# A two-layer metaformer on one core: where the first sample's spectral result is loaded from, and the order of the loads at the seam between two stages

## The chip, the cores and the metric

The kernel runs on one core of a Trainium2 chip, in float32. The metric is device time in microseconds of one execution. Each kernel is run several times and the median is given. Beside that, one execution is recorded by the hardware profiler. Its span goes from the first to the last instruction; its own time is a little longer than the span.

## The reference

The input is 16 samples of 128 channels by 32 x 32 positions. Layer 0 is a linear attention followed by a spectral filter over the 1024 tokens; layer 1 is a pair of 3 x 3 convolutions followed by a routed expert layer.

```python
# layer 0
x = x + attention(ln_c(x))                     # 4 heads, softmaxed q and k, 1x1 projections
t = to_tokens(x)                               # 16 x 1024 x 128
u = ln_t(t)
# spectral part: causal convolution with 16 filters phi (plain and sign-alternated), then a matrix per filter
out = sum_k conv(phi_k, u) @ (s_k * M_phi_plus_k) + sign * conv(phi_k, sign * u) @ (s_k * M_phi_minus_k)
out = out + sum_i shift(u, i) @ M_u_i          # 3 taps
t = t + weighted sum over 4 prefixes of the sequence
# layer 1
x = x + relu(bn2(conv3x3(relu(bn1(conv3x3(ln_c(x)))))) + ln_c(x))
t = t + experts(ln_t(to_tokens(x)))            # 64 experts, each takes its top 8 tokens of each sample
```

## The kernel before

Layer 0's attention and the forward transform of the spectral part run per sample (lines 221 to 774). They leave each sample's spectrum in DRAM (`vd`), its partial result in DRAM (`xd`), and the combined filter matrices in SBUF as `mst` (128 partitions x 32 x 128, 16 KB in each partition), which `filters` builds from 16 loads of `M_phi`.

The **spectral stage** (lines 777 to 921) runs over 16 chunks c of frequencies. `generate` makes the filter matrices of chunk c + 1 with TensorE (stationary `mst`, moving `ph`; line 817), `collect` copies them out of PSUM (828, 830), `multiply` applies those of chunk c to the spectra of all samples (841). In each chunk m runs over 0 to 3, and m takes the parts q = 2m and 2m + 1 of the next chunk's `generate`; part q reads rows 4q to 4q + 3 of `mst`. Each chunk needs spectra `xc`, which `fetch` loads (793) and `turns` on GpSimd turns into `v` (808, 809). `combine` (870, 871) and `finish` (855 to 858) make the results `ys`, and `finish` stores them to DRAM in two stores (862): `yd[0]` holds the 112 rows of chunks 0 to 13, `yd[1]` the 16 rows of chunks 14 and 15. `finish` of chunk c runs in the first step of chunk c + 1, on GpSimd; that of the last chunk runs behind everything, on VectorE. Within `ys` each result of sample 0 sits in 4 partitions for either r, 4 KB in each.

The **convolution stage** (from line 935) takes one sample after the other. Its buffers lie where those of the spectral stage were, and a buffer's first use waits for the last use of what lay there. For sample b, `load` brings x from `xd` and y from `yd` in two parts, 112 rows (896 KB) and 16 rows (128 KB); y has two buffers. Then follow the even and odd classes of the inverse transform (`even`, `odd_t` on GpSimd, 1049 to 1058; `odd_sd`, `odd_turn`, `odd_out` on VectorE, 1062 to 1079), `inverse` on TensorE with `wi` (1133), `add` (1140), tokens, statistics, norm, the product with `tmat` (`terms`, 1173), the transposed image, `ab` (1199), `pair` on GpSimd (1203), and the passes of the first convolution with the matrices `cw` (1013). For all these a planner (`planned`) has written out one order over all samples, with its costs and due times; the instructions of TensorE, VectorE, ScalarE and GpSimd, and SyncE's (SP's) transfers, then stand in that order on each engine. In it, sample 2's `odd_sd` and `odd_turn` stand on VectorE ahead of sample 0's `ab`.

`keep` puts matmuls of the identity, whose result nobody reads, on TensorE: 26 calls, each two instructions of the shape 128 x 256, ahead of the first sample's work (1509).

On SP, the transfers at the seam stand in this order: `gate_w`, `gate_b` (two), `tmat`, `wi`, the four stores of chunks 14 and 15, the last 16 rows of y(0), x(1), y(1), its last 16 rows, the two `cw`, four loads of biases, x(2), y(2) and its last 16 rows. x(0) and the first 112 rows of y(0) go out on GpSimd's queue.

## Time and profile before

| what | value |
|---|---|
| median of 4 runs | 1231.87 us (1226.96, 1227.6, 1236.75, 1236.15) |
| profiled execution: its own time | 1226.96 us |
| profiled execution: its span | 1225.1 us |
| mean granted clock of TensorE | 0.992 |
| TensorE matmuls, busy | 1154.5 us (94%) |
| VectorE / ScalarE / GpSimd, busy | 930.0 / 725.1 / 601.3 us |
| hardware DMA queue | 170.46 MB, 41.2% of 16 engines' span |
| filler matmuls at the seam | from 640.09 us, 11.49 us |
| first step on y(0) | 654.75 us |
| first instruction on y(2) | 675.36 us |
| first two paired convolution passes | from 679.84 us |

Times of single instructions are counted from the span's start. A busy TensorE is not yet a TensorE at its peak, since matmuls are pipelined, and the granted clock is the share of full speed that the array was given. An engine's idle time is put down to whatever ended it; where an instruction waits for several things, it is the last of them. A queue's wait (SPq) is the time in which the next transfer could not be issued; its landing is counted from its issue.

### The profile page before, as it was taken

To read this page: it belongs to the slowest core of one execution; us is meant where nothing else is said; L and a number is where in the kernel's file an instruction comes from. 1 tells how busy PE (TensorE), PEld (TensorE's weight loads), DVE (VectorE), ACT (ScalarE), POOL (GpSimd) and SP (SyncE) were. 2 spreads that over 40 slices of the span, in tenths; PEclk is the share of its full clock that TensorE was granted. 3 is DMA by queue.
4 is the path that set the end of the run, shared out by engine and by line. 5 is a ranking of instruction groups with operands and counts; after the bars stand their busy time and mean duration, and the time that the engine had idled before them with its cause. 6 is when DMAs were issued, how large, how long until landed. Compare 5 with 4: busy or idle time off the path is not lost.

```text
span 1225.1 us, 34369 instructions
## 1 busy us (share of the span) xinstructions
PE 1154.5 (94%) x14376; PEld 946.0 (77%) x14376; DVE 930.0 (76%) x1944; ACT 725.1 (59%) x1420; POOL 601.3 (49%) x800
## 2 busy tenths in 40 slices
PE   7889999999999999999997999999999999998995
PEld 4667767777777999999986888888888888886443
DVE  5888888888776677777764789898898989875235
ACT  4777777776655787877851446555556555644211
POOL 2436454665568788888872434344333333330003
PEclk9999999999999999999998999999999999999998
DMA  7004335253445244444348412233332331406998
GB/s 283 25 31 160 131 99 164 95 160 126 141 135 182 90 141 138 137 141 140 134 153 283 110 52 67 79 96 120 106 119 87 103 103 53 156 35 240 333 403 364
DMA packets 91243, 175.14 MB, mean 143 GB/s; under 512 B 5968, under 2 KB 42064, under 8 KB 90448
## 3 DMA queue, kind: packets, MB, share of 16 engines
q1 hardware_dynamic: 90448, 170.46, 41.2%
q8 instruction: 113, 1.85, 0.6%
q0 software_dynamic: 640, 2.49, 0.6%
q14 instruction: 42, 0.34, 0.1%
HBM read 110.28 MB, written 62.65 MB: 141 GB/s over the span
## 4 chain that ended last, share of the span: by engine, by line
PE 54%; DVE 22%; issue 11%; ACT 6%; DMA 4%; POOL 2%; SPq 0%; POOLq 0%; ACTq 0%; DVEq 0%
PE pcv L1013 10%; PE pg L817 10%; PE py L841 10%; PE big L639 6%; DVE bst L135 4%; PE big L172 3%; PE big L152 3%; PE big L571 3%; PE big L451 2%; PE big L534 2%; PE big L433 2%; DVE abss L1256 1%; DVE xp L1278 1%; DVE xp L1140 1%; ACT ub L550 1%
## 5 line engine op out<-in xcount | busy, mean ns | idle before, releaser
L1013 PE MATMUL pcv<-v,cw 128*128 128x256 f32 x1152 | 258.2, 380 | 0.9 <-POOL v L1203 0.9
L1013 PEld LDWEIGHTS pcv<-v,cw 128*128 128x128 f32 x1152 | 214.7, 190 | 34.0 <-issue 4.9
L830 ACT COPY g<-pg 128x512 f32<-128x512 f32 x316 | 161.1, 605 | 28.3 <-PE pg L817 27.5
L828 DVE COPY g<-pg 128x512 f32<-128x512 f32 x196 | 127.7, 682 | 65.0 <-PE pg L817 65.0
L817 PE MATMUL pg<-ph,mst 32*128 32x128 f32 x4096 | 137.4, 278 | 1.3 <-DVE x L646 0.9
L817 PEld LDWEIGHTS pg<-ph,mst 32*128 32x128 f32 x4096 | 125.1, 186 | 14.7 <-DVE g L828 7.7
L841 PE MATMUL py<-g,v 128*32 128x128 f32 x4096 | 125.1, 274 | 2.5 <-POOL v L809 1.8
L841 PEld LDWEIGHTS py<-g,v 128*32 128x32 f32 x4096 | 108.1, 110 | 10.7 <-POOL v L809 2.3
L144 ACT ACTIVATE tok<-tok,sts 128x128 f32<-128x128 f32 x256 | 101.9, 480 | 16.9 <-DVE sts L1090 13.6
L135 DVE BATCH_NORM_STATS2 bst<-big 128x6 f32<-128x256 f32 x256 | 91.1, 417 | 21.7 <-PE big L152 12.3
L808 POOL TENSOR_TENSOR v<-xc 128x256 f32<-128x256 f32 x128 | 96.9, 781 | 11.0 <-DMA xc<-vd 10.4
L639 PE MATMUL big<-u,mu 128*128 128x128 f32 (+4 forms) x384 | 86.0, 380 | 0.0
L1203 POOL TENSOR_TENSOR v<-abss 128x256 f32<-128x256 f32 x64 | 49.1, 787 | 68.1 <-DVE abss L1199 56.7
L287 POOL TENSOR_TENSOR xf<-ab 128x256 f32<-128x256 f32 x34 | 24.8, 728 | 110.3 <-DVE ab L254 110.2
L1222 POOL TENSOR_TENSOR yo<-abss 128x256 f32<-128x256 f32 x32 | 23.6, 737 | 108.5 <-DVE abss L1218 108.5
L639 PEld LDWEIGHTS big<-u,mu 128*128 128x128 f32 x384 | 56.7, 191 | 18.0 <-issue 15.4
L571 PE MATMUL big<-wf,ub 128*128 128x256 f32 x256 | 62.0, 385 | 0.2
L144 ACT ACTIVATE tt<-tt,sts 128x128 f32<-128x128 f32 x128 | 51.1, 481 | 14.5 <-DVE sts L1090 14.5
L809 POOL TENSOR_SCALAR v<-v 128x256 f32<-128x256 f32 x64 | 55.1, 862 | 5.6
L476 POOL TENSOR_TENSOR ke<-ke,ks 128x1024 f32<-128x1024 f32 x16 | 30.6, 1914 | 55.0 <-DVE qs L484 43.4
L571 PEld LDWEIGHTS big<-wf,ub 128*128 128x128 f32 x256 | 46.2, 190 | 8.8 <-ACT xn L424 3.0
L915 ACT COPY yt<-py 128x512 f32<-128x512 f32 x60 | 35.2, 586 | 29.0 <-ACT g L830 14.9
(256 smaller groups left out, 2481.1 us busy)
## 6 DMA issues: line engine op xcount, KB each, us to landing
we<-in_weight SPq DMA_DIRECT2D x32, 1024.0 KB, 9.2
xc<-vd SPq DMA_DIRECT2D x64, 256.0 KB, 3.0
yd<-ys SPq DMA_DIRECT2D x32, 512.0 KB, 3.8
vd<-xf SPq DMA_DIRECT2D x15, 1024.0 KB, 5.1
y<-yd SPq DMA_DIRECT2D x15, 896.0 KB, 6.3
x<-in_x SPq DMA_DIRECT2D x16, 512.0 KB, 5.3
mi<-in_M_phi SPq DMA_DIRECT2D x16, 512.0 KB, 4.7
xd<-x SPq DMA_DIRECT2D x16, 512.0 KB, 6.4
```

The lines of the kernel that those rows point to most:

```text
L135: nc.vector.bn_stats(bst[:, j : j + 2, :].rearrange("p j s -> p (j s)"), src[:, j : j + 2, :].rearrange("p j c -> p c j"),)
L144: nc.scalar.activation(dst[:, j, :], src[:, j, :], AF.Identity, bias=nm[:, j : j + 1], scale=r[:, j : j + 1],)
L571: nc.tensor.matmul(dst, self.ub[:, q, :], wf[:, q, :], start=True, stop=True)
L639: nc.tensor.matmul(self.pa[:, a:hi], mu[:, NF - 1 - si, tap, :], self.u[:, a - tap : hi - tap], start=(tap == 0), stop=(tap == KU - 1),)
L808: nc.gpsimd.tensor_tensor(vv[:, x, 1:, bs], e, o, op)
L809: nc.gpsimd.tensor_scalar(v[:, :, 0, bs], v[:, :, 2, bs], -1.0, None, ALU.mult)
L817: nc.tensor.matmul(pg[r][:, i], mst[rs, 4 * q + i, :], ph[rs, c, :], start=True, stop=True,)
L828: nc.vector.tensor_copy(dst, src)
L830: nc.scalar.copy(dst, src)
L841: nc.tensor.matmul(py[rows, x, kl, :], v[:, (x * NM + m) * JL + jl, 1 - ri : 3 - ri, :] .rearrange("p k b -> p (k b)"), g[:, ((x * 2 + ri) ...
L1013: nc.tensor.matmul(pc[:, i], wt[:, dy, k, :], v[:, k, dy * WT : dy * WT + HT], start=(dy == 0), stop=(dy == 2),)
L1203: nc.gpsimd.tensor_tensor(v[:, k, WT : WT + HT], self.ab[:, 0], self.ab[:, 1], op)
```

## The change

- `mst` becomes two halves of 16 rows, each with the shape of one y buffer, in a pool `ypool` of two buffers under the tag "y". The y of the convolution stage takes its two buffers from this pool, no longer from `first`. So y(0) lies where rows 0 to 15 of `mst` were, and y(1) where rows 16 to 31 were.
- The first 112 rows of y(0) are loaded by SP within the spectral stage: in chunk 14, step m = 3, behind the last `xc` load.
- `finish` of chunks 14 and 15 copies sample 0's rows straight from `ys` into y(0): four copies of 16 KB for each chunk, ahead of the chunk's stores. Of chunk 15's four, two are issued by ScalarE, all others by SP. The stores of both chunks remain, as the other samples need them.
- x(0) moves from GpSimd's queue to SP, behind the last stores. Then follow the first 112 rows of y(1), x(1), and the last 16 rows of y(1) (before, x(1) stood ahead of y(1)).
- `tmat` moves behind these; `gate_w` and `gate_b` move behind the two `cw`, ahead of the biases.
- `keep` ahead of the first sample's work goes from 26 calls to 13.

```diff
+    ypool = ctx.enter_context(tc.tile_pool(name="ypool", bufs=2, reuse_waits="tile"))
+    yts = {}
+
+    def load_y(b, j0, j1):
+
+        if b not in yts:
+            yts[b] = ypool.tile([P, 2, 2 * NM, C], F32, name="y", tag="y", bufs=2)
+        i = j0 >= P - 2 * JL
+        k = j0 - i * (P - 2 * JL)
+        nc.sync.dma_start(
+            yts[b][j0:j1].rearrange("p r x e -> p r (x e)"),
+            yd[i][k : k + j1 - j0, :, b].rearrange("j r x e -> j r (x e)"),
+        )
...
-        mst = lconst.tile([P, EPR, C], F32, name="mst")
+        mst = [
+            ypool.tile([P, EPR // 2, C], F32, name=f"mst{i}", tag="y", bufs=2) for i in range(2)
+        ]
+
+        def mrow(i, n=1):
+            h, k = divmod(i, EPR // 2)
+            return mst[h][:, k : k + n]
...
-                            pg[r][:, i], mst[rs, 4 * q + i, :], ph[rs, c, :], start=True, stop=True,
+                            pg[r][:, i], mrow(4 * q + i)[rs, 0], ph[rs, c, :], start=True, stop=True,
...
+                for kl in range(JL // RG if c + 2 >= NCH else 0):
+                    for r in range(2):
+                        j0 = P + (c - NCH) * JL + kl * RG
+                        (nc.scalar if kl and c + 1 == NCH else nc.sync).dma_start(
+                            yts[0][j0 : j0 + RG, r].rearrange("p x e -> p (x e)"),
+                            ys[r * B :: 2 * B, kl].rearrange("p x m e -> p (x m e)"),
+                        )
                 for kl in range(JL // RG):
...
                             fetch(c + 2, 0)
+                            if c + 2 == NCH:
+                                load_y(0, 0, P - 2 * JL)
...
-        FIRST = ("wi", "v", "cw0", "cw1", "p1", "y")
+        FIRST = ("wi", "v", "cw0", "cw1", "p1")
...
-            (nc.sync if b else nc.gpsimd).dma_start(xt[b], xd[b])
-            yts[b] = first.tile([P, 2, 2 * NM, C], F32, name="y", tag="y", bufs=2)
-            for i, js in enumerate((slice(P - 2 * JL), slice(P - 2 * JL, P))):
-                (nc.gpsimd if b + i == 0 else nc.sync).dma_start(
-                    yts[b][js].rearrange("p r x e -> p r (x e)"),
-                    yd[i][:, :, b].rearrange("j r x e -> j r (x e)"),
-                )
+            if b != 1:
+                nc.sync.dma_start(xt[b], xd[b])
+            if b:
+                load_y(b, 0, P - 2 * JL)
+            if b == 1:
+                nc.sync.dma_start(xt[b], xd[b])
+            if b:
+                load_y(b, P - 2 * JL, P)
...
             for b in range(2):
                 load(b)
+            nc.sync.dma_start(tmat, io["tmat"])
             for n in range(2):
                 nc.sync.dma_start(cw[n], cwd[n])
+            nc.sync.dma_start(gw, io["gate_w"])
+            for j in range(2):
+                nc.sync.dma_start(gb[j * E : (j + 1) * E, :], io["gate_b"])
...
-            keep(ps, "cv", 26)
+            keep(ps, "cv", 13)
```

## The prediction

> **What bounds the kernel now.** First the page and the clock of the core, for the whole. TensorE works in nearly every slice. The slice that stands out is the 22nd (about 643 to 674 us): a granted clock of 8 tenths, and the largest DMA rate in the middle of the run. That is the seam between the spectral stage and the convolution stage, and all edits lie there.
>
> ```profile
> span 1225.1 us, 34369 instructions
> PE 1154.5 (94%) x14376; PEld 946.0 (77%) x14376; DVE 930.0 (76%) x1944; ACT 725.1 (59%) x1420; POOL 601.3 (49%) x800
> ...
> PEclk9999999999999999999998999999999999999998
> ```
>
> Then the chain of waits across the seam (start, length, what).
>
> ```profile
> 643.92 7.19 DMA yd<-ys
> ...
> 651.55 0.62 SPq L1036
> ...
> 654.13 9.79 DMA cw<-cwd
> 663.92 0.02 issue
> 663.94 11.33 DMA y<-yd
> ...
> 675.36 0.43 DVE z L1062
> ...
> 679.84 5.45 PE pcv L1013 x24
> ```
>
> Two transfers carry it: the last store of `yd`, and the y of the third sample (b=2), whose issue comes late. Third, TensorE's timeline: what the array does meanwhile.
>
> ```profile
> 640.09 11.49 PE L165 MATMUL wm<-ident 128*128 128x256 f32 x52
> 654.91 1.13 PE L1133 MATMUL big<-wi,y 128*128 128x128 f32 x8 [3.33 <-DMA y<-yd]
> ...
> 676.15 2.75 PE L1013 MATMUL pcv<-v,cw 128*128 128x256 f32 x12
> 679.84 5.45 PE L1013 MATMUL pcv<-v,cw 128*128 128x256 f32 x24 [0.94 <-POOL v L1203]
> ```
>
> The 52 are filler. From 680 us on the same view shows TensorE full (10.0 of 10 us in most stretches to 740), so an earlier first convolution is kept to the end, less what is lost on the way. Last, the waits of SP's queue, and the clock in stretches of 2 us.
>
> ```profile
> SPq L1036 <- DMA yd<-ys: 6.7, 1, 6.7
> SPq L1033 <- DMA cw<-cwd: 2.5, 1, 2.5
> ...
> SPq L1033 <- DMA y<-yd: 2.4, 1, 2.4
> SPq L1036 <- DMA cw<-cwd: 1.7, 1, 1.7
> ```
>
> ```profile
> 644.00:646.00 2.00, 2.00 (x11) 1.76 (x10) 0.00 (x0) 0.00 (x0) 0.00 (x0) 1.00 1.02 418
> ...
> 652.00:654.00 2.00, 0.00 (x0) 0.00 (x0) 0.00 (x0) 0.00 (x0) 0.00 (x0) 1.00 0.44 98
> ...
> 660.00:662.00 2.00, 2.00 (x11) 2.00 (x11) 0.00 (x0) 0.00 (x0) 0.00 (x0) 0.50 0.97 368
> ```
>
> The three short waits have a pattern: each ends when the transfer issued eight places earlier on SP lands. Counting from the last rows of y(0): y(1) is 3rd, cw 5th and 6th, x(2) 11th, y(2) 12th and 13th, x(3) 14th. x(2) waits for y(1), the 13th for the first cw, x(3) for the second cw. At the start of the run SP's 15th transfer waits for its 7th. So SP has eight transfers in flight.
>
> **The change, part by part.**
>
> *The head start.* Now DVE ends the results at 643.53; stores, their 7.2 us, the reload of 16 rows (issue 0.62, landing about 3.1) let the first even/odd step start at 654.75. The change copies rows out of `ys`: two issues of 0.32 on SP (two more on ACT, which idles until 667.50), done by 644.2. No row shows an SBUF to SBUF copy of 16 KB. Nearest are tmat (64 KB, 2.1 us) and gb (0.2 KB, 2.5 us); from above, a full 512 KB yd store, 3.8 us. I take 2.6, by the small ones: start 646.8, **7.95 earlier** (bounds 6.7 to 8.5). On size the Trainium skill speaks against it: DMA: Bandwidth & Descriptors, section Rules for kernel authors, says transfers under 64 KB pay mostly overhead and should be joined. No row before has this shape; by that rule the eight copies are dear in bandwidth, but the sum would stay, since it counts only a landing.
>
> *What must be there.* The large part of y(0) (896 KB) is issued behind the last `xc` load (SP, 627.16): after the yd store of generation 13, issued 622.76 with a landing of 3.8, so near 627.5; landing 6.3 to 10.3 gives 634 to 638, against a need of 646.8. It follows the `xc` load that releases POOL's turns (630.22) and the last multiplications (632.65): same queue, behind it, so 0 to 1.0 us; I take 0.2. wi stays near 632.7 and lands 6.6 later. x(0), now on SP behind the stores, is issued at 645.0; 1.5 MB at 415 GB/s plus 1.5 us is 650.5, needed by the add after 653.
>
> *Filler.* 26 fewer matmuls by 0.22 us: TensorE is free at 645.85, about 1 us before y(0). Cost nothing while the head start is there; if it slips, the gap grows as long.
>
> *Sample 0.* Inverse 0 takes 7.75 us now (654.91 to 662.66), partly at clock 0.50. Its vector chain alone ends at 659.82, 5.1 after its start; so 652.6 to 654.6 afterwards, and the chain to the copy of the image (676.08 now) at 666 to 668. Alone this would give 8 to 10 us.
>
> *SP's queue.* Four copies of generation 14 push its stores 1.3 us back; they still land before 644. Then: two copies, two stores (to 645), x(0), y(1), x(1), the last rows of y(1) (waiting for the stores, about 649, all SP's queue behind it), tmat, cw, cw, gw, gb, gb, four biases, x(2), y(2). tmat, gw and gb cost four issues (2.5 us), hidden behind data still moving. But gw and two gb now stand between cw and x(2): x(2) is exactly **eight behind the second cw**, not behind y(1). This is the new wait. Data through that cw: stores 1.05 MB, x(0) and x(1) 1.05, y(1) 1.05, tmat 0.07, cw 2.36, together 5.57 MB from about 645.5. The stores at 415 GB/s take 2.5; 4.52 MB at 339 (the mean from 654 to 666) take 13.3; plus 0.7 to landing: 662.0. All at 415 would be 659.6; at 283 (the mean over 652 to 676), 665.9.
>
> *y(2).* x(2) issues at 662.0, y(2) at 662.6. Median landing of such a y is 6.3, and x(2)'s 0.52 MB ahead costs 1.5: it lands at **670.4**, against 675.3 now (issued at 661.57, 13.4 behind the backlog). Bounds: 666.5 (cw at 659.6, nothing for x(2)) and 676.2 (cw at 665.9, and 8.2 to landing, the median in this stretch). It decides because DVE, whose order is fixed, does sample 2's odd parts (L1062 to L1068) ahead of `ab` of sample 0 (L1199), and POOL's pair and the two convolution passes at 679.84 wait for that. Sample 0 is ready at 666 to 668, so y(2) ends last: the convolution moves by 675.3 - 670.4 = **4.9**, not by 8 to 10.
>
> *The new gap.* The first pass (2.75 us) then ends near 671 and TensorE waits to about 675. Now, 3.33 us of idling are followed by clock 0.50 from 658 to 666. Two passes of 24 matmuls take 5.45; at half clock for some 3.4 us (the idle time that brought it on) 1.7 are lost, and sample 1's terms, waiting for ACT's norm, cover about 1. I add 0.7 (bounds 0 and 2.5).
>
> `mst` in two halves has the same matmuls (4096) and the same 16 vector instructions: nothing.
>
> **Sum.** -4.9 + 0.2 + 0.7 = -4.0 us. The profiled execution took 1226.96 (span 1225.1 and 1.86 around it): 1222.96. It is the fastest of four runs, 4.91 below their median of 1231.87; on that median **1227.9**.
>
> **Rivals.** *Full head start kept:* y(2) lands by 666, as when transfers run at over 400 GB/s or the eight-place limit does not bind x(2). For it: 418 and 419 in two stretches. Against: the mean of 339 from 654 to 666. The two chains then give -8 to -11; middle -9.5, 1222.4.
>
> *Hidden anyway:* the data rate stays near 283, y(2) lands at 674.3, and the 1.0 left goes into the gap's 0.9: 1231.8. For it: 199 GB/s from 670 to 674. Against: y(0)'s 0.9 MB no longer move in the seam.
>
> *Slower:* one mechanism, x(2) behind the second cw. It decides when the rate to that landing falls below 5.57 MB / 20.7 us = 269 GB/s, since then y(2) lands after 675.3. At 199, seen from 670 to 674, cw would land at 674.2, y(2) at 682.6, 7.3 late; TensorE idle for 10 us starts at half clock for 10 us, 5 more: 1244.2. Against: the same queue moved 4.26 MB of such data by 667.0.
>
> **How the numbers follow.** Forecast 0.52, full head start 0.28, hidden 0.10, slower 0.10. A run of this kernel tells about 1% (12.3 us) from no change, the four runs spreading over 9.8. Faster by over 1% (below 1219.6) takes the better part of the full head start, with the scatter: 0.20. Slower (above 1244.2) takes half of the slower case and some scatter: 0.08. Within 1%: 0.72. The forecast's own range is 1223 to 1231 (y(2) at 666.5 to 674). The range for 8 in 10, with the full head start less half its tail and the runs' scatter of some 4 each way, is 1218 to 1237.
>
> **What would show it.** Right: first even step near 647; a wait of SP before x(2) put down to cw, ending near 662; y(2) used near 670; convolution passes at 675; TensorE idle some 4 us before them, clock below 1. Wrong: even 0 after 649 (the copies are slow); x(2) issued before cw lands (no limit of eight); the convolution passes before 671 (y(2) was no bound) or after 680; or TensorE losing time after 685 that it does not lose now.

## The result, and the profile after

The changed kernel takes 1235.67 us (median of 53 runs, 1231.03 to 1245.56), the kernel before 1233.55 us (79 runs, 1226.96 to 1244.47). The ratio is 1.0023, 95% interval 1.0013 to 1.0032: about 2.8 us slower. The forecast said 4.0 us faster. The time lies within the range that was given, which is 19 us wide; the direction is wrong.

The profiled execution of the changed kernel took 1236.7 us. That of before, at 1226.96, turned out to be the fastest of its 79 runs, so the two profiles differ by 9.7 us where the kernels differ by 2.8. A second profile of each was therefore taken (c1, 1240.82, of the kernel before; c2, 1235.41, of the changed one), and stretches of time are compared over two profiles each.

The page of the changed kernel:

```profile
span 1234.9 us, 34327 instructions
PE 1157.3 (94%) x14350; PEld 947.6 (77%) x14350; DVE 930.7 (75%) x1944; ACT 725.2 (59%) x1420; POOL 601.1 (49%) x798
...
PEclk9999999999999999999997899999999999999998
```

The dent in the clock at the seam is still there, and there are two digits below 9 where there was one. The chain of waits across the seam (start, length, what):

```profile
634.39 0.87 issue
635.26 8.00 PE py L861 x221
...
646.64 0.52 SPq L882
647.20 0.50 SPq L882
648.44 4.29 DMA yd<-ys
652.83 10.97 DMA y<-yd
663.92 0.43 DVE z L1091
...
670.18 0.61 SPq L85
670.83 9.40 DMA y<-yd
```

The reload of y(0) is gone from it, but the store of `yd` is not: the last 16 rows of the *second* sample's y wait for it now (issue 652.83, after 4.29 us of store), and then come 11 us of transfer. Behind it stands the same y(2) as before, issued at 670.18 instead of 661.57. TensorE's timeline:

```profile
635.26 7.98 PE L861 MATMUL py<-g,v 128*32 128x128 f32 x221 [0.87 <-issue]
643.17 5.88 PE L178 MATMUL wm<-ident 128*128 128x256 f32 x26
649.30 0.46 PE L1162 MATMUL big<-wi,y 128*128 128x128 f32 x2 [0.26 <-DMA y<-ys]
651.26 0.94 PE L1162 MATMUL big<-wi,y 128*128 128x128 f32 x6 [1.50 <-DMA y<-ys]
...
676.54 2.75 PE L1041 MATMUL pcv<-v,cw 128*128 128x256 f32 x12
684.79 8.14 PE L1041 MATMUL pcv<-v,cw 128*128 128x256 f32 x24 [5.50 <-POOL v L1232]
```

The first inverse starts 5.6 us earlier than before (649.30 against 654.91), the paired passes 5 us later (684.79 against 679.84), after 5.50 us of idling, and they take 8.14 us instead of 5.45. In the second profile of the changed kernel the idling is 3.81 us, and the passes take 5.45 us as before:

```profile
687.09 5.45 PE L1041 MATMUL pcv<-v,cw 128*128 128x256 f32 x24 [3.81 <-POOL v L1232]
```

SP's waits from 590 to 700 us:

```profile
SPq L1535 <- DMA y<-yd: 3.9, 1, 3.9
...
SPq L1062 <- DMA cw<-cwd: 2.6, 1, 2.6
SPq L1538 <- DMA xp<-xd: 1.7, 1, 1.7
SPq L1540 <- DMA cw<-cwd: 1.4, 1, 1.4
```

The wait that the prediction named is there: x(2) (line 1062) waits for the second `cw`, eight places ahead; `gate_b` (1535) waits for y(1) in the same way. The traces also show what these waits hang on: SP's 320 transfers in the kernel before use eight completion semaphores in turn, and where a transfer waits for the one eight places ahead, it waits for the earlier use of its own semaphore. So the limit that the prediction put down to SP is one of this program; that the queue itself has one, no run shows. Last, stretches of 2 us around the last results (clock, share of the DMA engines and GB/s are the last three columns):

```profile
634.00:636.00 2.00, 1.13 (x34) 0.86 (x29) 0.00 (x0) 0.00 (x0) 1.92 (x3) 0.92 1.01 426
636.00:638.00 2.00, 2.00 (x45) 2.00 (x40) 0.61 (x2) 0.37 (x1) 1.92 (x3) 0.50 0.09 29
638.00:640.00 2.00, 2.00 (x61) 2.00 (x57) 0.15 (x1) 0.21 (x1) 0.58 (x1) 0.73 0.02 6
640.00:642.00 2.00, 2.00 (x84) 2.00 (x79) 0.77 (x3) 0.54 (x2) 0.00 (x0) 1.00 0.18 53
...
646.00:648.00 2.00, 2.00 (x11) 1.76 (x10) 0.61 (x2) 0.00 (x0) 0.00 (x0) 1.00 0.03 8
```

From 636 to 642, in the last 10 us ahead of the end of the results (646.61), the DMA engines stand nearly empty. In the kernel before, whose results end at 643.53, they move 193 to 242 GB/s there:

```profile
636.00:638.00 2.00, 1.87 (x68) 1.60 (x60) 0.75 (x2) 0.37 (x1) 1.92 (x4) 1.00 0.46 193
638.00:640.00 2.00, 2.00 (x77) 1.89 (x68) 0.76 (x2) 0.37 (x1) 1.20 (x2) 1.00 0.69 217
640.00:642.00 2.00, 2.00 (x14) 1.71 (x10) 1.35 (x3) 0.37 (x1) 0.00 (x0) 1.00 0.82 242
```

Up to 639.3 that is in part `wi` (issued at 632.68), and from 638 on chunk 14's stores (from 637.98) and, on GpSimd's queue, x(0) and y(0) (637.89 and 638.51). In the changed kernel y(0) and `wi` are through by then, chunk 14's stores follow at 641.00, and x(0) stands on SP behind the copies of chunks 14 and 15, which wait for results; it goes out at 648.91.

Then the stretches in which the data ahead of x(2) is moved:

```profile
652.00:654.00 2.00, 1.44 (x7) 0.98 (x7) 1.97 (x3) 0.00 (x0) 2.00 (x3) 0.68 0.93 225
654.00:656.00 2.00, 1.46 (x7) 1.16 (x7) 1.38 (x4) 0.00 (x0) 1.00 (x2) 0.50 1.01 272
656.00:658.00 2.00, 2.00 (x11) 2.00 (x11) 0.46 (x2) 0.00 (x0) 0.00 (x0) 0.50 1.05 223
...
662.00:664.00 2.00, 0.07 (x1) 0.10 (x1) 0.08 (x1) 0.00 (x0) 0.04 (x1) 0.74 1.00 251
664.00:666.00 2.00, 2.00 (x10) 2.00 (x11) 2.00 (x5) 0.00 (x0) 2.00 (x3) 0.50 0.98 410
666.00:668.00 2.00, 1.69 (x8) 1.39 (x7) 1.90 (x5) 1.33 (x3) 1.43 (x3) 0.50 0.99 390
```

**Where the time went.** Marks that are the same in all kernels: S is the issue of chunk 13's store, R the end of the last result on VectorE, even the first even or odd step on y(0), Y1 and Y2 VectorE's first step on y(1) and y(2), F the first convolution block of 48 matmuls in a row. All in us, two profiles each:

| stretch | before | after | change predicted | change measured (means) |
|---|---|---|---|---|
| S to R (last chunk) | 20.8, 20.6 | 23.6, 22.4 | +0.2 | +2.3 |
| R to even | 11.2, 11.6 | 4.8, 4.8 | -7.95 | -6.6 |
| R to Y1 | 20.3, 19.7 | 17.3, 16.2 | | -3.3 |
| R to Y2 | 31.8, 33.2 | 33.7, 30.2 | -4.9 | -0.6 |
| Y2 to F | 16.5, 18.2 | 19.2, 16.5 | +0.7 | +0.5 |
| S to F (the sum of S to R, R to Y2, Y2 to F) | 69.1, 71.9 | 76.5, 69.1 | -4.0 | +2.3 |

+2.3 us from S to F stands beside the 2.8 us of the runs. Outside S to F both kernels do the same; F to the end scatters by 4 us between two profiles of the same kernel (533.3 and 537.5 before, 535.4 and 534.5 after).

### The profile page after: what moved, and what is told of

It is laid out like the page before. It is cut to its first block, busy times and chain, and to the rows that moved or that the text cites. A ratio compares the mean times of both kernels' runs of the same rounds, so it can differ in the third digit from the quotient of the medians.

```text
span 1234.9 us, 34327 instructions
## 1 busy us (share of the span) xinstructions
PE 1157.3 (94%) x14350; PEld 947.6 (77%) x14350; DVE 930.7 (75%) x1944; ACT 725.2 (59%) x1420; POOL 601.1 (49%) x798
## 3 DMA queue, kind: packets, MB, share of 16 engines
q0 software_dynamic: 256, 1.05, 0.3%
## 4 chain that ended last, share of the span: by engine, by line
PE 54%; DVE 22%; issue 10%; ACT 6%; DMA 4%; POOL 2%; SPq 0%; POOLq 0%; DVEq 0%; ACTq 0%
PE pcv L1041 10%; PE pg L837 10%; PE py L861 10%; PE big L659 6%; DVE bst L148 4%; PE big L185 3%; PE big L165 3%; PE big L591 3%; PE big L471 2%; PE big L554 2%; PE big L453 2%; DMA y<-yd 2%; DVE abss L1285 1%; DVE xp L1307 1%; DVE xp L1169 1%
## 5 line engine op out<-in xcount | busy, mean ns | idle before, releaser
L1041 PE MATMUL pcv<-v,cw 128*128 128x256 f32 x1152 | 260.9, 383 | 5.5 <-POOL v L1232 5.5
L850 ACT COPY g<-pg 128x512 f32<-128x512 f32 x316 | 161.1, 605 | 28.3 <-PE pg L837 27.5
L861 PEld LDWEIGHTS py<-g,v 128*32 128x32 f32 x4096 | 109.8, 111 | 11.4 <-POOL v L829 2.7
L157 ACT ACTIVATE tok<-tok,sts 128x128 f32<-128x128 f32 x256 | 101.9, 480 | 17.5 <-DVE sts L1119 14.2
L148 DVE BATCH_NORM_STATS2 bst<-big 128x6 f32<-128x256 f32 x256 | 91.1, 417 | 21.1 <-PE big L165 11.7
L1251 POOL TENSOR_TENSOR yo<-abss 128x256 f32<-128x256 f32 x32 | 23.6, 736 | 111.3 <-DVE abss L1247 111.3
L157 ACT ACTIVATE tt<-tt,sts 128x128 f32<-128x128 f32 x128 | 51.1, 481 | 14.5 <-DVE sts L1119 14.5
L1162 PE MATMUL big<-wi,z 128*128 128x128 f32 x384 | 51.5, 294 | 1.8 <-DVE z L1108 1.2
```

What stands on the lines that cost most here:

```text
L148: nc.vector.bn_stats(bst[:, j : j + 2, :].rearrange("p j s -> p (j s)"), src[:, j : j + 2, :].rearrange("p j c -> p c j"),)
L157: nc.scalar.activation(dst[:, j, :], src[:, j, :], AF.Identity, bias=nm[:, j : j + 1], scale=r[:, j : j + 1],)
L850: nc.scalar.copy(dst, src)
L861: nc.tensor.matmul(py[rows, x, kl, :], v[:, (x * NM + m) * JL + jl, 1 - ri : 3 - ri, :] .rearrange("p k b -> p (k b)"), g[:, ((x * 2 + ri) ...
L1041: nc.tensor.matmul(pc[:, i], wt[:, dy, k, :], v[:, k, dy * WT : dy * WT + HT], start=(dy == 0), stop=(dy == 2),)
L1162: nc.tensor.matmul(self.px[:, q * P : (q + 1) * P], zq, wi[:, q, r, :], start=(r == 0), stop=(r == 1),)
```

## The experiments

Two theories stood at the start. One: x(2), eight places behind the second `cw`, is held by the limit of eight. The other: no place in the queue matters, only the data that has to pass ahead of y(2). When both left something over, a third was formed on the transfer engines' empty time, and a fourth on the granted clock. Ratios are to the kernel before, with 95% intervals; the times between marks are from one profile for each variant. Each variant has a short label, by which the table at the end names it.

**Second profiles of both kernels (c1, c2).** No edit.

> The kernel before once more, for a second profile. The stretch from the issue of chunk 13's store to the last instruction of the spectral results took 20.8 us in the first profile (622.76 to 643.53), from there to the first use of y(2) 31.8. If both were usual, they come out within 1 us of that, whatever the moment at which the stretch begins; the beginning itself differed by up to 5 us among the kernels run so far, though nothing ahead of it was changed.

> The changed kernel once more, for a second profile. The same stretch took 23.6 us (623.05 to 646.62) and 22.7 to 26.6 in the four variants of it; theory E (the early load of y(0), right behind the last xc and followed by wi, delays TensorE's instructions and xc while the DMA engines are full) expects 22.5 to 24 again. If the 23.6 were a chance (the granted clock was 0.62 from 636 to 640), it comes out near 20.8.

1240.82 and 1235.41 us; their stretches are in the table above. The last chunk is longer and the even step earlier in both profiles of the changed kernel; R to Y2 scatters by more (3.5 us) than the kernels differ.

**Undoing the late gates in the changed kernel (r1).** `gate_w` and `gate_b` go out early, ahead of `wi`, as before, and no longer behind the two `cw`; `tmat` stays late:

```diff
+        nc.sync.dma_start(gw, io["gate_w"])
...
-            nc.sync.dma_start(gw, io["gate_w"])
```

> The changed kernel with the three loads of gate_w and gate_b back where they stood before the change (ahead of wi), so that x(2) is eight places behind the last rows of y(1) and no longer behind the second cw. In the changed kernel's profile x(2) is issued at 669.7, y(2) at 670.2, y(2) is used at 680.3 and the paired passes start at 684.8. Theory A (the eight places hold y(2) back): x(2) and y(2) go out near 665, y(2) is used 4 to 5 us earlier, the passes start near 680 and the time falls by 5 to 7 us against the changed kernel, to about 0.998 of the kernel before. Rival B (y(2) lands when all bytes ahead of it have been moved, whenever it is issued): only the pause of the transfers between 668 and 672 is saved, y(2) is used 2 us earlier, the time falls by about 2 us to 1.001. Rival C (y(2) is not the bound): no change, 1.002.

1.003 [1.0012, 1.0048]: no gain. x(2) goes out 15.7 us behind R instead of 23.1 and 21.8, and yet y(2) is used 29.6 behind R (33.7 and 30.2): from x(2)'s issue to there it is now 13.9 us instead of 10.6 and 8.4. Most of the wait moved from the queue's place to the transfer itself.

**The late gates alone, in the kernel before (c4).**

```diff
-        nc.sync.dma_start(gw, io["gate_w"])
...
             for n in range(2):
                 nc.sync.dma_start(cw[n], cwd[n])
+            nc.sync.dma_start(gw, io["gate_w"])
```

> The kernel before with one part of the change alone: gate_w and gate_b issued behind the two cw, ahead of the biases. x(2) then stands eight places behind the second cw instead of behind y(1). Theory A: x(2) is issued when that cw lands, about 6 us later than before (23.4 us behind the last results instead of 17.5), y(2) 6 later; it lands behind a shorter backlog, so it is used 2 to 3 us later, and the paired passes and the time go up by 2 to 3 us, 1.002. Rival B (bytes alone): y(2) is used at the same moment, the time stays at 1.000.

1.0068 [1.0044, 1.0091], some 8 us: alone, the three small transfers do harm. Here x(2) waits for `cw` (26.1 us behind R; 17.5 and 18.4 before) and Y2 goes to 36.8 (31.8 and 33.2 before):

```profile
SPq L1030 <- DMA cw<-cwd: 2.5, 1, 2.5
```

The limit of the eight semaphores is real and can be dear; in the changed kernel undoing it brings nothing. That the data ahead of y(2) takes as long there is how r1's profile reads, and not tried by itself.

**Less data ahead of y(2) (r2 in the changed kernel, d1 in the kernel before).** The second `cw` and the biases (with the gates in the changed kernel) go out behind x(2) and y(2):

```diff
-            for n in range(2):
-                nc.sync.dma_start(cw[n], cwd[n])
+            nc.sync.dma_start(cw[0], cwd[0])
...
                     if b > 1:
                         load(b)
+                    if b == 2:
+                        nc.sync.dma_start(cw[1], cwd[1])
```

In the changed kernel:

> The changed kernel with the second cw (1152 KB, first needed by sample 0's second convolution near 700 us), the gate loads and the biases issued behind x(2) and y(2). A: nothing holds x(2) but its place; it goes out when y(2)'s buffer is free (659), y(2) is used near 671 to 673, passes from about 677, time 7 to 9 us below the changed kernel, 0.996 of the kernel before. B gives nearly the same, since 1.2 MB fewer bytes stand ahead of y(2) (3 to 5 us at 250 to 400 GB/s, and the pause of 2): 674, passes from 679, 0.998. C: no change, 1.002, or slower if the second cw comes late for sample 0's second convolution.

0.9963 [0.994, 0.9986]. In the kernel before:

> The kernel before with the second cw and the biases issued behind the third sample's x and y, nothing else moved. Theory that bytes ahead of the second y's successor set the start of the convolution: 1.5 MB less ahead of y(2) is 6 us at 250 GB/s; y(2) from 32.5 to about 27 us behind the results, the next holder is y(1) or the sample order, so the start moves by 3 to 5 us and the time is 0.996 to 0.9975 of before. Then the same gain as with the changed kernel (0.9963) shows that the change has no part in it. The rival that the order of issue does not matter, since all goes through the same engines: 0.999 to 1.001.

0.9968 [0.9945, 0.9991]. Both gain, and equally, so the gain is not the change's. With 1.4 MB less to pass, Y2 comes 27.3 us behind R in both. That fits y(2) as what holds the convolution; the next run takes that apart.

**Not waiting for y(2) (r3, d2).** In the changed kernel, the order of VectorE and GpSimd takes sample 2's even and odd steps behind sample 0's `mids`:

```diff
+        late = [(2, n) for n in ("even", "odd_sd", "odd_t", "odd_turn", "odd_out")]
+        order = [k for k in order if k not in late]
+        at = order.index((0, "mids")) + 1
+        order[at:at] = late
```

> The changed kernel with sample 2's five even and odd steps moved in the written order from ahead of sample 0's ab to behind its mids; no transfer moves. If y(2), through VectorE and GpSimd, is what holds sample 0's convolution (A and B alike), the paired passes start at 677 to 679 right behind the first pass, the idle 5.5 us and the half clock in the passes (8.1 us for 24 matmuls) go, and the time falls by 5 to 8 us against the changed kernel, 0.996 to 0.998 of the kernel before; if y(2) is then still late for sample 2's inverse, by 3. C: the passes start at 684 as they did, or the time stays at 1.002.

0.999 [0.9971, 1.001], some 4 us less than the changed kernel, where 5 to 8 were expected. The paired passes stand right behind the first one (36 matmuls from 27.8 us behind R), so it was y(2) that kept them. But sample 2 is then late itself, Y2 39.8 us behind R. With the second `cw` behind y(2) as well, and sample 1's steps moved too:

> The changed kernel with the second cw, gates and biases behind x(2) and y(2), and the order in which VectorE and GpSimd take the samples changed too: sample 1's parts behind sample 0's scales, sample 2's behind sample 0's mids. Theory that the head start of the first sample is real and is spent waiting for later samples' y in the order of VectorE: with the order changed too the first blocks start 5 or more us earlier than in the changed kernel and the time is 0.991 to 0.995 of before. The rival that the chain of sample 0 itself, or the second cw now behind, is the next bound: 0.996 or above, as with the second cw moved alone.

0.9989 [0.9968, 1.001], where 0.991 to 0.995 was expected, and by the middle of the interval worse than the second `cw` alone. The order written out for the kernel before is not a simple loss; Y2 is 39.7 us behind R here, so the likely place of the missing gain is sample 2.

**y(1) on GpSimd's queue (r4).**

```diff
-                load_y(b, 0, P - 2 * JL)
+                load_y(b, 0, P - 2 * JL, nc.gpsimd if b == 1 else None)
```

> The changed kernel with the large part of y(1) (896 KB) issued by GpSimd, on its own queue, as y(0) was before the change; nothing else moves. Before the change 644 to 648 ran at 415 GB/s with y(0) on GpSimd's queue beside the stores on SP's, and in the changed kernel 652 to 664 runs at 223 to 272 GB/s with all on SP's. Theory D (one queue alone moves y slowly, two side by side run at over 330 GB/s): y(1) is used by 657 to 659 instead of 663.9, the second cw lands 4 us earlier, the passes start near 680, 0.998 of the kernel before. Rival (all queues share the same engines and the rate is that of the data): y(1) within 1.5 us of 663.9, time within 1.5 us, 1.001 to 1.003.

1.0015 [0.9997, 1.0033], not conclusive: GpSimd, free of work, issued y(1) at 638.46 already, 16 us ahead of R. The last chunk (S to R) grew to 26.5 us, and Y2 came 27.5 behind R: in this profile one took what the other gave.

**The early load of y(0) undone in the changed kernel (c3).** Its 112 rows go out on SP behind chunk 14's stores, 3 us ahead of R; the gates stay late:

```diff
+                if c + 2 == NCH:
+                    load_y(0, 0, P - 2 * JL)
...
-                                load_y(0, 0, P - 2 * JL)
+                                load_y(0, 0, 0)
```

> The changed kernel with the 112 rows of y(0) loaded behind chunk 14's stores instead of ahead of wi, about where GpSimd loaded them before the change; all else as changed. Theory E: the stretch from chunk 13's store to the last results falls from 23.6 to 21 us, the idle time of TensorE put down to issue in it from 0.9 (up to 2.5 in a variant) to 0.4, and the time falls by 2 to 3 us, to 1.000 of the kernel before; y(0) then lands near the last results plus 3 to 4, so the first even step comes no later than in the changed kernel (4.8 behind them). Rival (the stretch's length is chance or comes from the extra issues on SP): 23 us again and 1.002. A cost: if y(0) lands late, the first even step comes 2 us later and half of the gain is gone.

1.0039 [1.0021, 1.0056], against 1.0023 [1.0013, 1.0032] for the same with the early load: no gain. The last chunk is back at 21.6 us (23.6 and 22.4 with the early load); R to Y2 is 33.2, within what the changed kernel's two profiles show. What is saved ahead of R does not reach the end.

**The early load alone, in the kernel before (e1).** `mst` in halves and the early 112 rows; the other 16 rows reloaded, and all else, as before.

```diff
                             fetch(c + 2, 0)
+                            if c + 2 == NCH:
+                                load_y(0, 0, P - 2 * JL)
```

> The kernel before with one part of the change: y in a pool of its own and its first 112 rows loaded on SP's queue behind the last generation; the last 16 rows are still read back after the stores, and x(0), the order of the loads and the gates' transfers are as before. Theory of the early load's price (bytes laid under the last chunk's results cost it 2 us): issue of the last chunk's store to the end of the results goes from 20.7 to about 23 us, even where nothing else is changed; 0.9 MB less stands ahead of the second y, which gives back 3 to 4 us at 250 GB/s, so the first convolution blocks start 1 to 2 us earlier on net and the time is 0.998 to 1.000 of before. The rival that an early load is hidden (my prediction's 0.2 us): the last chunk stays at 20.8 us, and the time is 0.9965 to 0.9975 of before.

0.9992 [0.9969, 1.0015]: nothing that is clear of noise. S to R 23.6 us (+2.9), R to Y2 28.6 (-3.9 against the mean of before). The prediction's 0.2 us for the early load was far too low, and its gain behind R was real.

**The copies alone (e2).** The changed kernel with y(0)'s 112 rows and x(0) on GpSimd's queue, and the order of the loads and gates as before:

```diff
-            if b != 1:
-                nc.sync.dma_start(xt[b], xd[b])
...
+            (nc.sync if b else nc.gpsimd).dma_start(xt[b], xd[b])
+            load_y(b, 0, P - 2 * JL, None if b else nc.gpsimd)
```

> The changed kernel without its early load: y(0)'s first 112 rows and x(0) on GpSimd's queue behind the last generation as in the kernel before, the gates' transfers and the two orders of x and y as before; only the 16 rows straight from the results are kept. Theory of the early load's price: if GpSimd's transfers land behind the last results, the last chunk is back at 20.8 us; the first even step waits for the 112 rows, 6 to 9 us behind the results instead of 4.8; the bytes ahead of the second y are those of before. Time 0.998 to 1.001 of before. The rival that the copies themselves are dear (the last six issues of 0.5 to 0.95 us stand in the way): the last chunk stays at 22.5 to 23.5 us and the time is at 1.003 or above.

0.9979 [0.9959, 1.0]: a small gain at most. S to R 20.2 us; the even step 6.6 us behind R instead of 11.4, for the same rows and without the early load; Y2 31.0 behind R.

So neither half costs anything by itself that is clear of noise, and the whole costs 2.8 us. What is left of the change is x(0), which went from GpSimd's queue to SP's, and small parts that no run takes alone: y(1) ahead of x(1), the late `tmat`, and the halves side by side.

**x(0) alone back on GpSimd's queue, in the changed kernel (f1).**

```diff
             if b != 1:
-                nc.sync.dma_start(xt[b], xd[b])
+                (nc.sync if b else nc.gpsimd).dma_start(xt[b], xd[b])
```

> The changed kernel with x(0) alone back on GpSimd's queue; early load, copies, order and gates stay as changed. Theory that the lost prefetch on GpSimd's queue decides (there x(0) starts some 6 to 8 us ahead of the last results, with transfers engines that otherwise stand empty; on SP's it stands behind the last stores as 0.5 MB more ahead of the second y's): the second y lands about 2 us sooner than in the changed kernel, and the time is 0.998 to 1.0005 of before. The rival that the early load of y(0) and its slow-down of the last chunk are what costs, wherever x(0) goes: 1.0015 to 1.003, like the changed kernel.

0.9962 [0.9936, 0.9987]: this one line turns the change into a gain. From the ends of the two intervals it is worth 3 to 12 us; the medians (1232.51 us, and 1234.19 for the kernel before beside it, 0.9986) speak for the lower end. GpSimd's timeline has the transfer 11 us ahead of R (652.63):

```profile
641.60 0.62 POOL L1062 DMA_DIRECT2D xp<-xd  x1
```

and the stretches that were empty are full, at a price: TensorE stands still from 641.8 to 644.9.

```profile
642.00:644.00 2.00, 0.00 (x0) 0.00 (x0) 0.15 (x1) 0.00 (x0) 0.22 (x1) 1.00 0.62 158
644.00:646.00 2.00, 1.11 (x41) 1.11 (x44) 0.00 (x0) 0.00 (x0) 0.00 (x0) 0.99 0.88 332
646.00:648.00 2.00, 2.00 (x48) 2.00 (x42) 0.76 (x2) 0.37 (x1) 0.00 (x0) 0.50 0.92 342
```

S to R is 27.0 us, R to Y2 26.4, x(2) goes out 16.0 us behind R (23.1 and 21.8 in the changed kernel). The one profile shows Y2 53.3 us behind S, within what the changed kernel's two show (57.3, 52.6); that there is a gain rests on the runs, and this profile does not show where it comes from.

The Trainium skill, page DMA: Bandwidth & Descriptors, section Issuing engines are not separate DMA queues, says that starting transfers from several engines saves only the time to start them, since all run on the same 16 engines. Here the runs put the move at 3 us or more, where x(0)'s issue takes 0.6 us on GpSimd and 1.0 on SP. The likely reason is that an engine's queue is also an order, and that SP's stood behind transfers that waited for results; this is argued from the rows above, and no run took it apart.

**The same move alone, in the kernel before (f2).**

```diff
-            (nc.sync if b else nc.gpsimd).dma_start(xt[b], xd[b])
+            nc.sync.dma_start(xt[b], xd[b])
```

> The kernel before with x(0) alone moved from GpSimd's queue to SP's, behind the last stores. Theory of the lost prefetch: 0.5 MB more between the last results and y(2), so 1 to 2 us more to the convolution's first blocks, 1.001 to 1.003 of before. The rival that x(0)'s queue is of no account: 0.999 to 1.001.

0.9972 [0.9946, 0.9998]: faster, where a loss was expected. Here SP waits for its last stores anyway before it can reload y(0)'s 16 rows, and x(0) moves in that hole. Without x(0) beside them, the stores land sooner too: the reload goes out 5.2 us behind R instead of 8.0 and 8.4. And y(0) leaves GpSimd 9.3 us ahead of R here, instead of 5.0, so two loads moved and not one. So the queue is not good or bad in itself. A reading that fits both runs is that the transfer should fill time in which the DMA engines would stand empty: on SP in the kernel before, on GpSimd in the changed one, in which SP has no such wait left to fill. It is a reading, not shown by itself.

**Both corrections together (f3), and without the early load (f4).** The changed kernel with x(0) on GpSimd and the second `cw`, gates and biases behind y(2):

> The changed kernel with x(0) on GpSimd's queue and the second cw, the gates and the biases behind x(2) and y(2). If the two costs are separate (x(0)'s queue, and the second cw ahead of y(2)), their gains add: 0.993 to 0.9955 of before. If with the second cw behind y(2) something else holds the convolution (y(1), or sample 0's own chain), x(0)'s move adds little to the 0.9963 of the second cw moved alone.

0.9954 [0.993, 0.9978]. The gains do not add fully (0.9962 and 0.9963 alone); S to R is 26.8 us here too. The copies alone, without the early load, with the second `cw` and the biases behind y(2):

> The copies of the last 16 rows straight from the results without the early load (y(0)'s other rows and x(0) on GpSimd's queue as before), with the second cw and the biases behind x(2) and y(2). Theory that the copies gain 2 to 3 us by themselves and the second cw's place 4 us, and that the early load is a loss: 0.993 to 0.996 of before, no slower than the same with the early load kept and x(0) on GpSimd's queue. The rival that the early load gains as much as it costs: the two are equal within the interval.

0.9926 [0.9903, 0.995], median 1225.33 us: the fastest of all, faster than both kernels, and no slower than the version with the early load. S to R 21.0 us, Y2 25.0 behind R. TensorE's timeline has the passes without a gap:

```profile
639.94 7.23 PE L863 MATMUL py<-g,v 128*32 128x128 f32 x256 [0.53 <-DVE pooled L959]
647.10 5.88 PE L180 MATMUL wm<-ident 128*128 128x256 f32 x26
...
678.27 7.94 PE L1047 MATMUL pcv<-v,cw 128*128 128x256 f32 x36
```

**The clock (g1, g2).** Over all runs the changed kernel has the lower mean clock: 0.985 (54 runs) against 0.990 (142 runs). Within each kernel 0.001 of clock goes with 0.9 to 1.1 us, so the clock by itself would account for 4.6 us, more than the whole loss. Is it cause or company? Matmuls without use were put into TensorE's waits:

```diff
+        warms = {(0, "inverse"): 10, (0, "tokens"): 12, (0, "convc"): 24}
...
+        def warm(count):
+            if count:
+                wm = ps.tile([P, P], F32, name="wm2", tag="s", bufs=1)
+            for _ in range(count):
+                nc.tensor.matmul(wm, ident, ident, start=True, stop=True)
...
```

In the changed kernel:

> The changed kernel with matmuls that compute nothing put into TensorE's waits at the start of the convolution stage: 11 of 128x128 (1.4 us) inside the first sample's inverse, 4 ahead of its odd part and of the second sample's, 10 behind it, 12 behind the first turn of tokens, 24 (3.2 us) behind the first convolution pass. Over the profiles so far the kernels in which TensorE waits longest between the first sample's even step and the third sample's y (25 to 29 us: 0.985 to 0.986) have the lowest mean clock, those with 16 to 21 us the highest (0.990). Theory that half clock behind these waits is most of the change's loss: the mean clock rises from 0.985 to 0.988 or more and the time falls from 1.0023 to 0.997 to 1.000 of before. The rival that the half clock falls where TensorE is not on the path, and the time is all bytes: the clock rises, the time stays at 1.001 to 1.0035.

The clock rose as meant, to 0.991 over 12 runs, above that of before. The page no longer has the dent:

```profile
span 1235.5 us, 34587 instructions
...
PEclk9999999999999999999999999999999999999998
```

The time is 1.0016 [0.9997, 1.0036], 0.9 us less than without the fillers, with an interval that includes none. In the timeline the passes run at full speed (5.45 us; without fillers 8.14 and 5.45), and start no sooner (37.3 us behind R; 38.2 and 34.7 without), since GpSimd's pair, which waits for y(2), lets them go no sooner:

```profile
681.30 5.52 PE L1056 MATMUL wm<-ident 128*128 128x128 f32 x48
687.75 5.45 PE L1041 MATMUL pcv<-v,cw 128*128 128x256 f32 x24 [0.93 <-POOL v L1244]
```

The control, the kernel before with such fillers:

> Control: the kernel before with such matmuls in its waits (the run of 26 ahead of the first inverse made 36, 4 ahead of the two odd parts, 10 behind the first inverse, 14 behind the first convolution pass). Its mean clock is 0.990 already: if half clock is what the changed kernel loses by, this one has less to gain, clock 0.991 to 0.993 and 0.9975 to 1.000 of before. If matmuls of this kind help both alike, the clock is not what sets the two kernels apart.

Clock 0.993, time 0.9996 [0.9979, 1.0013]. So the clock is more likely company than cause: with the clock of the kernel before or a higher one the changed kernel is still at 1.0016 by the middle of the interval. The intervals of g1 and of the changed kernel leave room for a gain of all 2.8 us and for none, and the fillers may cost something themselves, so this is not shown. That half clock in the waits costs little would fit, since y(2) ends those waits whatever the clock is. The Trainium skill, page TensorE: Matmul & The Clock Gate, section Terms, puts the penalty at the time spent at the lower clock times the share that is lost. By that rule the 0.0045 of clock between the two kernels (0.985 against 0.990, unrounded) over 1234 us would be 5.6 us, an estimate; the runs show some 0.9 for a rise of 0.006, at the ends of both intervals together some 4.

**All kernels together.** For the 16 kernels whose sample order is unchanged, the time goes with S to Y2 (correlation 0.89, 1.25 us of time for 1 us), and not with S to Y1 (0.27):

| kernel | ratio | S to R | S to Y1 | S to Y2 | clock, mean of the runs |
|---|---|---|---|---|---|
| copies alone, second cw behind (f4) | 0.9926 | 21.0 | 36.8 | 46.0 | 0.990 |
| after, x(0) on GpSimd, second cw behind (f3) | 0.9954 | 26.8 | 40.7 | 48.0 | 0.989 |
| after, x(0) on GpSimd (f1) | 0.9962 | 27.0 | 40.8 | 53.3 | 0.990 |
| after, second cw behind (r2) | 0.9963 | 22.6 | 39.5 | 49.9 | 0.989 |
| before, second cw behind (d1) | 0.9968 | 20.5 | 40.4 | 47.8 | 0.990 |
| before, x(0) on SP (f2) | 0.9972 | 21.6 | 38.8 | 48.9 | 0.991 |
| copies alone (e2) | 0.9979 | 20.2 | 36.3 | 51.2 | 0.988 |
| early load alone (e1) | 0.9992 | 23.6 | 41.4 | 52.2 | 0.991 |
| before, fillers (g2) | 0.9996 | 20.3 | 40.0 | 52.4 | 0.993 |
| before (two profiles) | 1 | 20.7 | 40.7 | 53.2 | 0.990 |
| after, y(1) on GpSimd (r4) | 1.0015 | 26.5 | 40.5 | 54.1 | 0.988 |
| after, fillers (g1) | 1.0016 | 22.7 | 39.0 | 55.5 | 0.991 |
| after (two profiles) | 1.0023 | 23.0 | 39.7 | 54.9 | 0.985 |
| after, gates early (r1) | 1.003 | 23.1 | 38.7 | 52.6 | 0.986 |
| after, y(0) behind chunk 14's stores (c3) | 1.0039 | 21.6 | 38.2 | 54.8 | 0.985 |
| before, gates late (c4) | 1.0068 | 21.1 | 41.6 | 57.9 | 0.986 |

The change brings Y1 1.0 us closer to S and puts Y2 1.8 us further away, and the time follows Y2. What has to pass from S to Y2 is the same amount: 12.7 and 12.9 MB before, 12.9 and 12.4 MB after. By their busy share, the DMA engines stand empty for 12.6 and 12.0 us of it before, and for 14.5 and 13.6 after; 12.6 with x(0) on GpSimd, 8.3 with the copies alone. Over the 16 kernels this goes with the time too, but less (correlation 0.71): with the gates early in the changed kernel (r1) it is 11.2 us, and that kernel is among the slow ones.

**What stays open.** The gates early in the changed kernel (r1) and x(0) on GpSimd (f1) lie off that line, 3.7 us above and 5.5 us below; with one profile each, and 1 to 5 us between two profiles of a kernel, this can be scatter, and was not settled. By the medians alone f1 would lie some 2.5 us below. So it is shown that x(0)'s place decides the sign of the change, and not shown how.

## Why the prediction was wrong, step by step

The step that failed is the largest term of the sum: y(2) was to come 4.9 us sooner, and it came 0.6 sooner. Beside it the early load, taken at 0.2 us, cost 2.3. Between them they turn -4.0 into +2.3.

- **The bound: right.** The convolution starts when the third sample's y is there; r3 and the table show it. So the head start of the first sample is spent in waiting, as was said, and not worth 8 to 10 us.
- **The new wait: right in kind.** x(2) behind the second `cw`, eight places ahead; the eight are the program's semaphores and not SP's own limit. It was put at 18.5 us behind the last result (662.0 against 643.5); measured 23.1 and 21.8.
- **The rate to that `cw`: mis-sized, and the main failure.** 5.57 MB were to pass with 4.52 MB at 339 GB/s. The `cw` landed where 273 and 292 GB/s over the 5.57 MB put it, close to the lower bound that the prediction named (283), and above the 269 at which its slower rival begins. That 339 was the mean of a stretch in which the two loads of `cw` made up more than half of the data. In the changed kernel the 2 us stretches from 652 to 664, mostly x and y, ran at 223 to 272 GB/s, those from 664 to 668, mostly `cw`, at 410 and 390, the engines' share being near 1.0 in all. And y(2) then took 10.6 and 8.4 us, against 8.4 in the sum. Together Y2 moved by -0.6 instead of -4.9, in the means; the two profiles of a kernel differ by 1.4 and 3.5 us.
- **The early load: mis-sized.** Taken at 0.2 us (bounds 0 to 1.0), it costs 2.3 to 2.9 from S to R, in the changed kernel and alone (e1). The prediction only looked at the queue's next load; it left out that TensorE itself stands still, for 0.87 and 1.05 us in the changed kernel's two profiles and 2.6 us in e1, with no transfer of data that it waits for; what ends these stretches stands in the last section.
- **x(0)'s move: missed.** It was counted as 0.5 MB more in the queue's sum. What was not weighed is that on GpSimd's queue it runs ahead of the last results (by 5.6 us in the kernel before, 11.0 in f1), while SP's queue is headed by copies that wait. That line alone is 3 to 12 us (f1), and by it the sign of the whole; by what path stays open, since f1's last chunk grew by 4 us and its y(2) came no sooner behind S than the scatter allows.
- **The head start:** 6.6 instead of 7.95 us. The issues took longer than the 0.32 us that the sum used: 0.5 us each on SP, 1.35 and 0.51 on ScalarE. An effect on the end is not to be expected, since y(2) decides.
- **The gap and the clock:** forecast 0.7 us. The gap came, with 5.50 us and 2.7 lost in the passes in one profile, with 3.81 and nothing lost in the other; g1 puts the clock's part at about 0.9 us, with none and all of the loss inside the interval. The sum let half clock last as long as the idling that brought it on; the profile before has it from 658 to 666 behind 3.33 us of idling, so this was not read from a row.

Of the rivals, "hidden anyway" came closest for y(2): at 283 GB/s it left 1.0 us of the 4.9, and 0.6 was measured. "Slower" had the direction, but by x(2)'s place in the queue, and with the gates early (r1) x(2) went out 6 to 7 us sooner without a gain. The rest of the loss, the early load's price and x(0)'s place, stood in no rival.

## What to carry to other kernels

Before moving a transfer to another queue, list what stands ahead of it there and what that waits for: a queue headed by transfers that wait for results moves nothing, and a second engine's queue can then be worth more than its issue time. Try such a move by itself: here it gained in one kernel what it lost in its neighbour. A head start for the first consumer is worth only what the last needed transfer gains; count the data up to that transfer, at the rate of its own kind of load. And when a lower clock goes with longer waits, fill the waits before blaming the clock.

## What the runs showed of the hardware

- With more data laid under the last chunk, it tended to take longer, and TensorE had more idle time there that ended with nothing but its own issue. S to R with 3.5 to 3.7 MB (before, e2, f4, d1, g2): 20.2 to 21.0 us, no such idle time; c3, with 3.6 MB too, 21.6 and 1.0; with 4.0 MB (c4) 21.1 and 0.3; with 4.5 MB (after, r1, r2, r3, d2, g1, f2): 21.6 to 23.6 us, 0.9 to 1.9 us idle; with 5.0 MB (e1): 23.6 and 2.6; with 5.4 MB (r4): 26.5 and 3.1; with 5.9 MB (f1, f3): 27.0 and 26.8, 3.8 and 3.7. In r4, f1 and f3 the mean granted clock of the stretch was 0.94, in the first profile of the changed kernel 0.93, in all others 1.00, so half clock is a part of their length.
- All 20 of these idle stretches of 0.25 us or more (14 profiles) end 1.2 to 1.6 us behind the end of a packet of 16 KB on the instruction queue (q8 of the profile's DMA queues); in f1 the packet starts at 642.59, inside the idle stretch that ends at 644.89. So TensorE most likely waited for its instructions. That full DMA engines are what delays these packets was not tried.
- At a full share of the DMA engines, stretches of mostly x and y moved 223 to 272 GB/s and those of mostly `cw` 390 to 410 (the rows of the changed kernel from 652 to 668).
- SBUF to SBUF copies of 16 KB: 0.5 us to issue on SP, 1.35 and 0.51 on ScalarE; the first even step came 2.9 us behind the end of the last issue. The rule on small transfers that the prediction weighed spoke against them; the copies alone show no loss (0.9979).
- The same move of one transfer, x(0) from GpSimd's queue to SP's, gained 0.3% in the kernel before (f2) and cost 0.6% in the changed one (1.0023 against f1's 0.9962; by the medians some 0.3%).
